# First layer's context attention and feed-forward in a two-layer decoder: another order of a batch's steps

## The chip, the cores and the metric

The kernel runs on one core of a Trainium2 chip, in one launch. The metric is the device time in microseconds (us), from runs of the whole program; lower is better. All arithmetic is in fp32.

Five engines work beside each other, each through its own queue in order: TensorE (PE in the profile; PEld is its weight load), VectorE (DVE), ScalarE (ACT), GpSimd (POOL) and SyncE (SP, which here only issues DMAs). An engine that waits for another holds everything queued behind the waiting instruction. [...]

## The reference

The input is x of 8 batches x 512 tokens x 256, and a context of 8 x 64 x 256 with a mask. Two decoder layers follow, each with self-attention, context attention and a feed-forward part, each part with a residual sum and a layer norm behind it. The change concerns the second and third part of the first layer:

```python
x = _layernorm(x + _L0_xattn_ref(x, ctx_1024, ctx_1024, mask))
#   16 heads of 16; q, k, v are x and the context as they are, no projections:
#   sim = q k^T / sqrt(16) + NEG_BIAS * (1 - mask); out = softmax(sim) v
x = _layernorm(x + _L0_ffn_ref(x, ...))
#   h = gelu(butterfly(x @ W_exp + b_exp) + up_bias)      256 -> 1024
#   y = butterfly(h) @ W_con + b_con + down_bias          1024 -> 256
```

The butterflies are linear; the kernel folds them into the two matrices earlier, so that the feed-forward part is a product with a 256 x 1024 matrix (`wup`), a Gelu, and a product with a 1024 x 256 matrix (`wdn`).

## The kernel before

A batch's 512 tokens are 4 tiles (`NT`) of 128 rows; 256 channels are 2 chunks (`KC`) of 128. The stage `l0_context_ffn` (L1107) works batch after batch in a loop (L1150) with one turn for each (batch, tile). It overlaps two batches: while the context attention of batch b runs, the feed-forward part of batch b-1 or b-2 is taken off a list `pieces`, a few at a time. The order on every engine is that in which the Python code emits the instructions; nothing reorders them.

The steps of the context attention, by their functions:

- `l0x_scores(b, i)` (L700): 8 small products on PE into two PSUM tiles `s_xs` (L708), in an order in which the first two go to the first tile and the next two to the second. Then on DVE two additions of the mask bias, one for each tile (L721), the maximum of each head (L729), and on POOL the subtraction of it (L730). The result is `p`.
- `l0x_exps(b, i)` (L740): one Exp on ACT, in place in `p`. `l0x_sums` (L743): the sums of each head, on DVE (L746).
- `l0x_transposes(b, i)` (L949): 8 transposes of `p` on PE into two PSUM tiles `tP` (L957), each copied by ACT to `pt` (L958).
- `l0x_values(b)` (L960): 8 products on PE for the whole batch into one PSUM tile `s_xpv` (L966), copied by two ACT copies to `oT` (L975); then the context of batch b+2 is fetched by DMA.
- `l0x_back(b)` (L980): 4 reciprocals of the sums on DVE (L985), 8 transposes `tO` on PE (L995), the scaling by the reciprocals on DVE (rx, L997), the residual sum on POOL (rx, L1003), the layer norm's statistics on DVE (L237, L238, then ve at L248) and a power on POOL (L249). The scaling of the layer norm, one short DVE step (ve, L253) and four ACT steps (L257), is put on a list `backs`.
- `l0x_keys(b)` (L692): two POOL operations that spread the context of batch b (bd, L684), a DMA for its mask, and a DVE step for its bias (L154).
- `turned_x(b)` (L672): 8 transposes of x into two PSUM tiles (`tT`, L678), copied by ACT (L679).

The steps of the feed-forward part, from `ffn(b)` (L1008): the transposes of x to `xF`, then 16 pieces. Eight `up` pieces make the first-matrix products, one PSUM tile `s_h` each (4 products of 512 columns, L1015), with a Gelu on ACT behind each (`gate`, L1022). Eight `down` pieces make the second-matrix products into two PSUM tiles `o_out` (L1039); on DVE the residual sum (r, L1049) and the statistics follow; the scaling goes to a list `ends`. `plus` (L1024) is a POOL operation that prepares the residual. `some(n)` takes up to n pieces, `run(queue)` takes the first entry of a list.

PSUM is split (L946) into 2 tiles of two banks (`s`: `s_xs` and `s_xpv`), 3 tiles of one bank (`t`: `tP`, `tO`, `tT`, even `s_h`, first `o_out`) and 1 tile of one bank (`o`: odd `s_h`, second `o_out`). A step that needs a tile waits until its last reader is done:

```python
ctx.enter_context(psum("b", 2, 3, 1))
# in l0x_scores
ss = [s_tile("s_xs") for _ in range(2)]
# in l0x_values
s = s_tile("s_xpv")
```

Exp and Gelu use different tables of ACT, and a table load (`ACT_TABLE_LOAD`) stands in ACT's queue at each change between them; copies and the layer norm's scaling have none. In the loop before, each turn has the scores of one tile, the sums and transposes of the tile before it, two pieces, the Exp, and two more pieces. At tile 0 the turn also has `l0x_values` of the batch before and `l0x_keys` of the next, at tile 1 `l0x_back`, at tile 2 the scaling from `backs`, `turned_x` of the next batch and `ffn`, at tile 3 `plus`.

The stage before this one and the second layer behind it are the same in both kernels. After the loop the rest of `pieces` is run, with the first steps of the second layer among the last twelve.

Of the kernel before, what the change touches and what calls it, by code (L numbers as in the profile page):

```python
# [50 lines left out]
def decoder_kernel(ctx: ExitStack, tc: tile.TileContext, a: dict, out: bass.AP):  # L51
# [640 lines left out]
    def l0x_keys(b):  # L692

        bd = ph.tile([P, KC, 8, S2], F32, tag="bd", name="bd")
        for c in range(KC):
            l0x_spread(b, c, bd[:, c])
        l0x_mask(b)
        l0x_bias(b)

    def l0x_scores(b, i, p=None, by=None):  # L700


        xT, bias = live["xT", b], live["bias", b]
        ss = [s_tile("s_xs") for _ in range(2)]
        for c in range(KC):
            for r in range(4):
                quarter = slice(32 * r, 32 * r + 32)
                pe.matmul(  # L708
                    ss[r // 2][:, r % 2, c * P : (c + 1) * P],
                    lhsT=xT[quarter, c, i * P : (i + 1) * P],  # L710
                    rhs=live["bd", b, c][quarter, 2 * r : 2 * r + 2].rearrange("p h k -> p (h k)"),
                    start=True,
                    stop=True,
                )
        if p is None:
            p = ph.tile([P, 16, S2], F32, tag="p", name="p", bufs=4)
        mx = col("mx16", 16)
        live["p", b, i] = p

        def add(j):  # L720
            dve.tensor_tensor(  # L721
                p[:, 8 * j : 8 * j + 8].rearrange("p (r h) k -> p r h k", r=2),
                ss[j][:, :, 0 : 2 * P].rearrange("p r (h k) -> p r h k", k=S2),
                bias[:, i, :].unsqueeze(1).unsqueeze(1).to_broadcast([P, 2, 4, S2]),
                ALU.add,
            )

        def less():
            dve.tensor_reduce(mx, p, AX.X, ALU.max)  # L729
            (by or pool).tensor_tensor(p, p, mx.unsqueeze(2).to_broadcast([P, 16, S2]), ALU.subtract)  # L730

        if by is None:
            add(0)
            add(1)
            less()
            return None
        add(0)
        return [partial(add, 1), less]
# [4 lines left out]
    def l0x_sums(b, i):  # L743
        if i == 0:
            live["sums", b] = early.tile([P, NT, 16], F32, tag="sums16", name="sums")
        dve.tensor_reduce(live["sums", b][:, i, :], live["p", b, i], AX.X, ALU.add)  # L746
# [202 lines left out]
    def l0x_transposes(b, i):  # L949
        pf = live["p", b, i].rearrange("p h k -> p (h k)")  # L950
        if i == 0:
            live["pt", b] = ph.tile([P, 8, S], F32, tag="pt", name="pt", bufs=1)
        pt = live["pt", b]
        for c in range(2):
            t = t_tile("tP")
            for h in range(4):
                pe.transpose(t[:, h, :], pf[:, (4 * c + h) * P : (4 * c + h + 1) * P], ident)  # L957
            (dve.tensor_copy if b == 0 and c else act.copy)(pt[:, 4 * c : 4 * c + 4, i * P : (i + 1) * P], t)  # L958

    def l0x_values(b):  # L960

        pt = live.pop(("pt", b))
        s = s_tile("s_xpv")
        for c in range(KC):
            for r in range(4):
                pe.matmul(  # L966
                    s[32 * r : 32 * r + 32, c, :],
                    lhsT=live["v2"][:, b % 2, 4 * c + r, :],
                    rhs=pt[:, 2 * r + c, :],
                    start=True,  # L970
                    stop=True,
                )
        oT = ph.tile([P, KC, S], F32, tag="oT", name="oT", bufs=1)
        for c in range(KC):
            act.copy(oT[:, c, :], s[:, c, :])  # L975
        live["oT", b] = oT
        if b + 2 < NB:
            l0x_context(b + 2)
# [128 lines left out]
    with phase("l0_context_ffn") as ph, tc.manual_schedule(engines=ALL):  # L1107
        wdn = ph.tile([P, 8, D], F32, tag="wdn", name="wdn", bufs=1)

        def wdn_piece(f):  # L1110
            t = t_tile("tW")
            for j in range(4):
                pe.transpose(t[:, j, :], wdnT[:, j % 2, (f + j // 2) * P : (f + j // 2 + 1) * P], ident)
            act.copy(wdn[:, f : f + 2, :].rearrange("p f n -> p (f n)"), t.rearrange("p j n -> p (j n)"))

        steps_ = [(b, i) for b in range(NB) for i in range(NT)]
        turn0, turn1, product0, product1, _ = unfinished

        def some(n):
            for _ in range(n):  # L1120
                if pieces:
                    pieces.pop(0)()

        def run(queue):
            if queue:
                queue.pop(0)()

        for n, aside in enumerate((nothing, turn0, turn1, nothing)):
            l0x_transposes(*steps_[n])
            aside()  # L1130
        for _ in parts:
            pass
        product0()
        l0x_values(0)
        product1()
        l0x_back(0)
        l0x_transposes(1, 0)
        for n in range(1, NT - 1):
            for f in range(4 * n - 4, 4 * n, 2):
                wdn_piece(f)  # L1140
            l0x_transposes(1, n)
        l0x_keys(2)
        live["xT", 2] = turned_x(2)
        run(backs)
        dve.tensor_tensor(upb, upb2, upb, ALU.add)
        for n in range(NT - 1):
            l0x_sums(1, n)
        more = [slot(f"gate{n}") for n in range(2)]
        gates = [more[f // 4][:, f % 4 * S : (f % 4 + 1) * S] for f in range(8)]
        for n in range(2 * NT, len(steps_) + 3):  # L1150
            b, i = n // NT, n % NT
            if n == 3 * NT:
                wqT = slot("wqT").rearrange("p (c n) -> p c n", c=KC)
                kd_ku = slot("kd_ku")
                wkdT = kd_ku[:, 0:256].rearrange("p (c n) -> p c n", c=KC)
                wkuT = kd_ku[:, 256:1280]
                wvuT = slot("vu")[:, 0:1024]
                tabs = slot("tabs")
                cs = tabs[:, 0:1024].rearrange("p (t n) -> p t n", t=2)
                causal = tabs[:, 1024:1536]  # L1160
                sp.dma_start(out=wqT, in_=rows(a["at_wqT"]))
                sp.dma_start(out=wkdT, in_=rows(a["at_wkdT"]))
                sp.dma_start(out=wkuT, in_=a["at_wkuT"])
                sp.dma_start(out=wvuT, in_=a["at_wvuT"])

                sp.dma_start(out=cs[:, 0, :], in_=a["rope"][0])
                for h in range(0, P, 32):
                    sp.dma_start(out=cs[h : h + 32, 1, :], in_=a["rope"][1][h ^ 32 : (h ^ 32) + 32, :])
                sp.dma_start(out=causal, in_=a["causal"])
            first = n == 2 * NT  # L1170
            if i == 2:
                run(backs)
            if n < len(steps_):
                l0x_scores(b, i)
            if n <= len(steps_):
                l0x_sums(*steps_[n - 1])
                l0x_transposes(*steps_[n - 1])
            if first:
                ffn(0)
                run(pluses)  # L1180
                run(ends)
            if i == 1:
                run(ends)
            if i == 1 and b > 1:
                l0x_back(b - 1)
            some(2)
            if i == 0:
                l0x_values(b - 1)
            if n < len(steps_):
                l0x_exps(b, i)  # L1190
            if i == 2 and b + 1 < NB:
                live["xT", b + 1] = turned_x(b + 1)
            some(2)
            if i == 0 and b + 1 < NB:
                l0x_keys(b + 1)
            if i == 3:
                run(pluses)
            if i == 2 and b > 1:
                ffn(b - 1)
        since = 0  # L1200
        while len(pieces) > 3 * NT:
            run(pieces)
            since = since + 1 if ends else 0
            if since == 3:
                run(ends)
                run(pluses)
        turned = slot("turned").rearrange("p (two j n) -> p two j n", two=2, j=2)
        sooner = [partial(l1_turn, 0, 0), partial(l1_turn, 0, 1), partial(l1_latent, 0)]
        for c in range(2):
            sooner.extend([partial(l1_query, 0, c), lambda c=c: (l1_key(0, c), l1_rope(0, c))])  # L1210
        run(sooner)
        while pieces:
            run(sooner)
            run(pieces)
# [997 lines left out]
```

## Time and profile before

| | |
|---|---|
| median of 3 runs | 3152.14 us (3150.56 to 3152.29) |
| profiled execution, its own time | 3156.77 us |
| its span, first to last instruction | 3155.1 us |
| granted TensorE clock, mean over the span | 0.990 |
| PE busy | 3063.9 us (97%) |
| DVE / ACT / POOL busy | 1920.7 / 1642.3 / 1101.3 us |
| first and last `s_xs` products of the loop's batches 2 to 7 | about 720.9 to 960.3 us |

Times within the profile are counted from the span's start. A line of the timeline gives the start, the time from there to the end of the merged instructions, the engine, the line of the kernel, the operation, output and inputs, the count, and in brackets the idle time ahead of it and what ended that. [...] An fp32 product of the code appears as two entries in PE's counts. Some matmul records can be missing.

### The profile page before, as it was taken

The page shows a single profiled execution, that of the slowest core. Times are in us where ns is not written, and L with a number is a line of the kernel's source. Part 1 is how long each engine was busy: PE and PEld are TensorE (multiplying, and loading weights), DVE is VectorE, ACT ScalarE, POOL GpSimd, SP SyncE. Part 2 cuts the span into 40 slices and gives each one's busy share as a digit, 9 for nine tenths or more (in the row PEclk, how much of TensorE's full clock was granted, in tenths as well). Part 3 has the DMA queues.
Part 4 walks back from the last instruction along what each step waited for, and adds up shares of the span by engine and source line. Part 5 has one row for each costly group of instructions (what it writes and reads, how often), then busy time and mean ns, then how long its engine had stood idle before and what let it go on. Part 6 is the DMA issues. An engine that isn't in the chain of part 4 may idle for free.

```text
span 3155.1 us, 54217 instructions
## 1 busy us (share of the span) xinstructions
PE 3063.9 (97%) x19598; PEld 2029.3 (64%) x19598; DVE 1920.7 (61%) x6331; ACT 1642.3 (52%) x3507; POOL 1101.3 (35%) x992
## 2 busy tenths in 40 slices
PE   8999999999999999999999999999999999999995
PEld 3444444455666677677767765666666558888885
DVE  6888888876553767767677746766766773110112
ACT  4555555557664666766676656555545543222222
POOL 5988888934432222222222210011111112221222
PEclk8999999999999999999999999999999999999998
DMA  5000111101006963333332310000000016766674
GB/s 165 28 28 28 41 45 44 35 6 43 6 3 170 255 132 48 41 41 41 42 45 38 42 43 1 16 16 25 22 18 21 21 51 210 226 193 180 185 238 148
DMA packets 170975, 235.25 MB, mean 75 GB/s; under 512 B 31915, under 2 KB 134059, under 8 KB 170709
## 3 DMA queue, kind: packets, MB, share of 16 engines
q1 hardware_dynamic: 144692, 179.91, 18.2%
q0 software_dynamic: 25584, 51.57, 11.5%
q8 instruction: 155, 2.54, 0.3%
q14 instruction: 112, 0.91, 0.1%
q10 hardware_dynamic: 432, 0.33, 0.0%
HBM read 136.03 MB, written 61.12 MB: 62 GB/s over the span
## 4 chain that ended last, share of the span: by engine, by line
PE 83%; DVE 6%; ACT 4%; DMA 2%; SPq 2%; issue 1%; POOL 0%; POOLq 0%; DVEq 0%; ACTq 0%
PE o_y L1975 7%; PE s_h L1958 7%; PE s_sc L480 5%; PE s_sc L1560 4%; PE o_pv L1345 4%; PE s_sc L1283 4%; PE tP L1332 4%; PE o_pv L576 4%; PE o_out L1369 4%; PE o_out L1039 3%; PE o_pv L1602 3%; PE s_q L1080 3%; PE o_qkv L1525 3%; PE tP L1592 3%; PE s_h L1015 2%; PE s_st L556 2%
## 5 line engine op out<-in xcount | busy, mean ns | idle before, releaser
L565 ACT ACTIVATE pt<-s_st 128x1024 f32<-128x1024 f32 x256 | 248.3, 1022 | 263.5 <-PE s_st L561 263.5
L1101 POOL DMA_DIRECT2D qk<-turned x256 | 202.8, 1168 | 520.2 <-PE tP L1332 319.4
L489 DVE CUSTOM_DVE_ANT_0 scored<-s_sc,decay 128x512 f32<-128x512 f32 x492 | 314.5, 686 | 54.3 <-PE s_sc L480 52.5
L1310 ACT ACTIVATE p<-p,nm 128x128 f32<-128x128 f32 (+3 forms) x512 | 282.6, 554 | 61.4 <-DVE nm L1296 61.4
L1263 DVE TENSOR_SCALAR p<-p,rsum 128x576 f32<-128x576 f32 (+4 forms) x768 | 297.1, 429 | 13.6
L1296 DVE CUSTOM_DVE_ANT_0 p<-s_sc,tabs 128x128 f32<-128x128 f32 (+3 forms) x512 | 215.6, 487 | 124.9 <-PE s_sc L1283 124.9
L1995 DVE TENSOR_SCALAR y<-o_y,share 128x256 f32<-128x256 f32 x71 | 34.2, 483 | 403.3 <-PE o_y L1975 403.3
L1958 PE MATMUL s_h<-xnT,we 128*128 128x256 f32 (+1 forms) x1248 | 258.8, 361 | 0.0
L1975 PE MATMUL o_y<-we,h 128*128 128x256 f32 x1136 | 251.4, 379 | 0.0
L1996 POOL DMA_INDIRECT total<-y,to x71 | 109.8, 1546 | 386.2 <-DVE y L1995 193.4
L1570 ACT ACTIVATE p<-s_sc,nm 128x576 f32<-128x576 f32 x256 | 187.4, 737 | 101.8 <-DVE nm L1564 101.1
L1975 PEld LDWEIGHTS o_y<-we,h 128*128 128x128 f32 x1136 | 215.3, 190 | 29.0
L1958 PEld LDWEIGHTS s_h<-xnT,we 128*128 128x128 f32 x1248 | 215.4, 190 | 23.9 <-ACT xnT L1937 0.2
L1564 DVE TENSOR_REDUCE nm<-s_sc 128x1 f32<-128x576 f32 x256 | 181.4, 750 | 73.2 <-PE s_sc L1560 73.2
L1332 PEld LDWEIGHTS tP<-ident,p 128*128 128x128 f32 x1280 | 144.8, 141 | 82.6 <-PE s_sc L1283 41.7
L480 PE MATMUL s_sc<-k,q 32*128 32x512 f32 x1024 | 188.9, 648 | 6.0 <-DVE mx L489 4.9
L1794 POOL DMA_INDIRECT rows_in<-z,irow x64 | 63.2, 988 | 374.2 <-DVE hit L1789 267.1
L1560 PE MATMUL s_sc<-k,q 64*128 64x288 f32 x1024 | 174.2, 433 | 9.7 <-ACT p L1570 9.7
L1332 PE MATMUL tP<-ident,p 128*128 128x128 f32 x1280 | 175.2, 276 | 0.1
L1937 ACT ACTIVATE xnT<-tZ,gb 128x256 f32<-128x256 f32 (+1 forms) x78 | 42.6, 546 | 237.5 <-PE tZ L1936 237.5
L1283 PE MATMUL s_sc<-qk 64*128 64x128 f32 (+3 forms) x1024 | 157.5, 443 | 3.8 <-DMA qk<-turned 3.3
L1965 ACT ACTIVATE h<-s_h 128x1024 f32<-128x1024 f32 x71 | 72.7, 1024 | 155.7 <-PE s_h L1958 155.7
(341 smaller groups left out, 6456.0 us busy)
## 6 DMA issues: line engine op xcount, KB each, us to landing
we<-in_mo_w SPq DMA_DIRECT2D x78, 1024.0 KB
rows_in<-zero SPq DMA_DIRECT2D x64, 530.0 KB
qk<-turned POOLq DMA_DIRECT2D x256, 128.0 KB, 4.3
coef<-in_ff_upw SPq DMA_DIRECT2D x40, 256.0 KB
coef<-in_ff_dnw SPq DMA_DIRECT2D x40, 256.0 KB
xr<-rows_in SPq DMA_DIRECT2D x32, 265.0 KB
x<-in_x SPq DMA_DIRECT2D x8, 512.0 KB
total<-x SPq DMA_DIRECT2D x8, 512.0 KB
```

The costliest lines, as they stand in the source:

```text
L480: pe.matmul(pairs[h // 2][:, h % 2, :], lhsT=q[r, i * P : (i + 1) * P], rhs=k[r, :], start=True, stop=True)
L489: dve.tensor_tensor_reduce(out=rows_[h], in0=pairs[h // 2][:, h % 2, :], in1=decay[:, i, :], scale=1.0, scalar=-3.0e38, op0=ALU.mult, op1= ...
L565: act.activation(pt, s, AF.Exp, scale=1.0 / 16.0)
L1101: pool.dma_start(out=qk[h : h + 32], in_=other[g : g + 32], accum_op=ALU.add)
L1263: dve.tensor_scalar(p[:, j, 0:n], p[:, j, 0:n], rsum[:, j : j + 1], None, ALU.mult)
L1283: pe.matmul(ss[j][:, at : at + n], lhsT=qk[h : h + 64, 0, i * P : (i + 1) * P], rhs=qk[h : h + 64, 1, 0:n], start=True, stop=True,)
L1296: dve.tensor_tensor_reduce(out=p[:, j, :], in0=ss[j], in1=causal[:, S - (i + 1) * P : S], scale=-1.0 / 8.0, scalar=3.0e38, op0=ALU.add, op ...
L1310: act.activation(p[:, j, :], p[:, j, :], AF.Exp, bias=nm[:, j : j + 1], scale=-1.0, accum_out=sums[:, j : j + 1])
L1332: pe.transpose(t[:, n, :], p[:, j, at * P : (at + 1) * P], ident)
L1560: pe.matmul(s[:, t, :], lhsT=q[h : h + 64, i * P : (i + 1) * P], rhs=k[h : h + 64, at : at + HALF], start=True, stop=True)
L1958: pe.matmul(s[:, j, :], lhsT=w1[:, c, f * P : (f + 1) * P], rhs=xnT[:, c, :], start=(c == 0), stop=(c == KC - 1),)
L1975: pe.matmul(o, lhsT=h[:, f, i * P : (i + 1) * P], rhs=w2[:, f, :], start=(f == 0), stop=(f == 7),)
```

## The change

The loop over (batch, tile) becomes a loop over batches with the order of a batch written out. In the first half of a batch the last two transposes of the batch before, then the four score steps of this batch, with the eight `up` pieces, `l0x_values`, `l0x_keys` and `l0x_back` among them; then `turned_x` and the four exponentials, one behind the other. In the second half four `down` pieces, the transposes of tiles 0 and 1 with the other four `down` pieces around them, `ffn` and `plus`, and the sums of tiles 2 and 3. The products, tiles and buffers are the same.

```diff
         gates = [more[f // 4][:, f % 4 * S : (f % 4 + 1) * S] for f in range(8)]
-        for n in range(2 * NT, len(steps_) + 3):
-            b, i = n // NT, n % NT
-            if n == 3 * NT:
+        for b in range(2, NB + 1):
+            if b == 3:
                 wqT = slot("wqT").rearrange("p (c n) -> p c n", c=KC)
...
                 sp.dma_start(out=causal, in_=a["causal"])
-            first = n == 2 * NT
-            if i == 2:
-                run(backs)
-            if n < len(steps_):
-                l0x_scores(b, i)
-            if n <= len(steps_):
-                l0x_sums(*steps_[n - 1])
-                l0x_transposes(*steps_[n - 1])
-            if first:
+            own = [partial(l0x_scores, b, i) for i in range(NT)] if b < NB else [nothing] * NT
+            if b == 2:
+                own[0]()
+                l0x_sums(1, NT - 1)
+                l0x_transposes(1, NT - 1)
                 ffn(0)
                 run(pluses)
                 run(ends)
-            if i == 1:
-                run(ends)
-            if i == 1 and b > 1:
-                l0x_back(b - 1)
+            else:
+                for i in range(2, NT):
+                    l0x_transposes(b - 1, i)
+                own[0]()
             some(2)
-            if i == 0:
-                l0x_values(b - 1)
-            if n < len(steps_):
+            l0x_values(b - 1)
+            own[1]()
+            some(2)
+            if b + 1 < NB:
+                l0x_keys(b + 1)
+            run(ends)
+            l0x_back(b - 1)
+            own[2]()
+            some(2)
+            own[3]()
+            some(2)
+            if b + 1 < NB:
+                live["xT", b + 1] = turned_x(b + 1)
+            if b == NB:
+                run(backs)
+                some(4)
+                ffn(b - 1)
+                break
+            for i in range(NT):
                 l0x_exps(b, i)
-            if i == 2 and b + 1 < NB:
-                live["xT", b + 1] = turned_x(b + 1)
+            some(4)
+            l0x_sums(b, 0)
+            l0x_transposes(b, 0)
+            run(backs)
             some(2)
-            if i == 0 and b + 1 < NB:
-                l0x_keys(b + 1)
-            if i == 3:
-                run(pluses)
-            if i == 2 and b > 1:
-                ffn(b - 1)
+            l0x_sums(b, 1)
+            l0x_transposes(b, 1)
+            some(2)
+            ffn(b - 1)
+            run(pluses)
+            for i in range(2, NT):
+                l0x_sums(b, i)
         since = 0
```

## The prediction

> **What bounds the kernel now.** First the page: which engine is full, and what the chain of waits that ended last consists of.
>
> ```profile
> PE 3063.9 (97%) x19598; PEld 2029.3 (64%) x19598; DVE 1920.7 (61%) x6331; ACT 1642.3 (52%) x3507; POOL 1101.3 (35%) x992
> PE 83%; DVE 6%; ACT 4%; DMA 2%; SPq 2%; issue 1%; POOL 0%; POOLq 0%; DVEq 0%; ACTq 0%
> ```
>
> TensorE (PE) is full and carries 83% of the chain. An edit that only reorders can gain no more than PE's idle time in the stretch that it reorders. That stretch runs from about 724 to 985 us. Next the busy time by windows, one window of 43 us in it (columns: window, length, then busy us of PE, PEld, DVE, ACT, POOL, then the granted clock, DMA share, GB/s), and the groups of ScalarE's table loads over 724 to 985:
>
> ```profile
> 767.00:810.00 43.00, 41.73 (x238) 27.12 (x236) 25.08 (x50) 29.36 (x41) 18.12 (x13) 1.00 0.03 5
> L1022 ACT ACT_TABLE_LOAD x19 | 24.4, 1283 | 7.0 <-PE s_h L1015 6.7
> L741 ACT ACT_TABLE_LOAD x18 | 23.1, 1283 | 0.3
> ```
>
> PE lacks 1.27 us in 43, ACT 13.64. ACT's 37 table loads (six a batch) are mostly off the path. Where PE waits is seen in PE's timeline of one batch:
>
> ```profile
> 769.25 1.92 PE L966 MATMUL s_xpv<-pt,v 128*32 128x512 f32 x16
> 771.10 3.70 PE L1015 MATMUL s_h<-xF,wup 128*128 128x512 f32 x8
> 774.73 0.73 PE L708 MATMUL s_xs<-bd,xT 32*128 32x128 f32 x16
> 775.39 1.09 PE L957 MATMUL tP<-ident,p 128*128 128x128 f32 x8
> 776.79 0.65 PE L995 MATMUL tO<-ident,oT 128*128 128x128 f32 x4 [0.31 <-ACT gate L1022]
> 777.84 0.66 PE L995 MATMUL tO<-ident,oT 128*128 128x128 f32 x4 [0.40 <-ACT pt L958]
> 778.33 7.13 PE L1015 MATMUL s_h<-xF,wup 128*128 128x512 f32 x16
> 786.05 1.09 PE L957 MATMUL tP<-ident,p 128*128 128x128 f32 x8
> 787.71 3.72 PE L1039 MATMUL o_out<-wdn,gate 128*128 128x256 f32 x16 [0.57 <-ACT gate L1022]
> 810.27 1.92 PE L966 MATMUL s_xpv<-pt,v 128*32 128x512 f32 x16
> ```
>
> A batch is 810.27 - 769.25 = 41.02 us. I read an operation's price as the distance to the next start. Eight tP cost 0.93 us where nothing is waited for (797.22 to 798.15), but 1.40 at 775.39 and 1.66 at 786.05; the first four tO cost 1.05, the second four 0.49. Waits of a batch: 0.47 + 0.56 + 0.73 = 1.76 us. All three are ACT being late with a PSUM tile, behind an exponential between two table loads. PE's own work is 41.02 - 1.76 = 39.26 us.
>
> **The change, part by part.** No instruction of PE, DVE or POOL is added or removed; ACT loses four of its six table loads a batch, 4 x 1.283 = 5.1 us.
>
> *Gain.* The exponentials no longer stand among the first-matrix products, so the three old waits can go: 1.76 us a batch, at most. What is late next is the pair of `s` tiles that a score step fills: there are only two such tiles, a step takes both, and s_xpv takes one. In the new order these steps stand closer together.
>
> *First new wait.* Score step 1 now follows s_xpv directly; before, two first-matrix pieces (3.6 us) lay between. Its second tile is the one that s_xpv filled and that ACT's two copies must empty:
>
> ```profile
> 771.29 1.07 ACT L975 COPY oT<-s_xpv 128x512 f32<-128x512 f32 x2 [1.05 <-PE s_xpv L966]
> ```
>
> The copies end at 772.36, 3.11 us after s_xpv's start, and PE follows 0.05 later (as after the gates above). PE would be there after 1.85 + 0.16 (the four of sixteen products that go to the free tile) = 2.01. Wait: 3.16 - 2.01 = 1.15 us. No row shows this pair of steps back to back. Bounds: 0.6, if one copy were enough; 1.7, if ACT came one gate (0.6) later.
>
> *Second new wait.* Step 3 needs step 2's additions, and on DVE these stand behind the whole of `l0x_back`: bias, ve, reciprocals, rx and statistics. The statistics wait for POOL's two sums rx, which stand behind step 1's subtraction and the two bd of `l0x_keys`. The rows:
>
> ```profile
> 775.49 1.29 DVE L721 TENSOR_TENSOR p<-s_xs,bias 128x512 f32<-128x512 f32 x2 [4.46 <-PE s_xs L708]
> 776.81 1.22 DVE L729 TENSOR_REDUCE mx<-p 128x16 f32<-128x1024 f32 x1
> 783.77 0.43 DVE L237 BATCH_NORM_STATS2 st<-rx 128x6 f32<-128x256 f32 x1
> 784.98 0.17 DVE L248 TENSOR_SCALAR ve<-mv 128x4 f32<-128x4 f32 x1
> ```
>
> ```profile
> 772.75 2.04 POOL L684 TENSOR_TENSOR bd<-ctxT,small 128x512 f32<-128x512 f32 x2
> 778.11 1.90 POOL L730 TENSOR_TENSOR p<-p,mx 128x1024 f32<-128x1024 f32 x1 [3.32 <-DVE mx L729]
> 781.25 2.50 POOL L1003 TENSOR_TENSOR rx<-rx,x 128x512 f32<-128x512 f32 x2 [1.23 <-DVE rx L997]
> ```
>
> Count from the end of step 1 on PE (775.39 in the old order). Maximum out: 778.03 - 775.39 = 2.64. Subtraction out: 780.01, so 4.62. Two bd: 6.66. Two sums rx: 9.16. The last two statistics and ve take 784.98 - 783.77 = 1.21 after the second sum, plus 0.05 and 0.08 between the steps: step 2's additions start at 10.50. The first is out after 0.68, the second 0.64 later; with 0.05 each, the tiles are free at 11.23 and 11.87. PE's way: two pieces 3.53, tO 0.95, step 2 0.66, two pieces 3.53, so 8.67 for the first tile and 8.83 for the second. Wait: 11.87 - 8.83 = 3.04 us. DVE's other work in this time is covered by POOL: a ve step held up by POOL's subtraction (0.96 us at 779.08 against 0.17 at 786.35, both ending with POOL's operation) ends at 4.65, reciprocals 0.5 and the first rx 0.68 make 5.8, before bd ends at 6.66. Bounds: 2.0 if one bd (1.02) were out of the way, 4.1 if one more stood in it.
>
> *Costed at nothing.* s_xpv needs the first tile of step 0. From the last second-matrix product, DVE takes 5.9 (r, statistics, then two sums of 1.13 that are now ahead, then an addition), plus 0.2 to start; PE takes xF 0.93, sixteen tP 1.86, step 0 0.66, two pieces 3.53 = 6.98. Slack 0.85; if gone, the excess is paid. The four exponentials: step 3's subtraction ends 5.1 after step 3 on PE, ACT's copies of xT at 5.6, one load and four exponentials to 11.1; PE comes to the first tP at 11.5, and needs only the first exponential (7.9). The scaling from `backs` (2.07) has 7.9 us of products before xF. Six PSUM tiles in a row at the batch's start go out at ACT's 0.535 against PE's 0.46: 0.1. The mask and context DMAs on SP keep their order and become due later than the tile they reuse; the layer-1 loads stay at the head of the fourth batch. After the loop the same 12 pieces are left.
>
> *Sum.* New waits 1.15 + 3.04 + 0.10 = 4.29, less 1.76: +2.5 us a batch. From s_xpv at 728.23 to that at 972.75 there are six batches. The last has no bd and no bias: POOL's sums start when tO and rx are out (about 5.0 after step 1, against 6.66), so some 1.7 less, +0.8. Five times 2.5 and 0.8: +13.3 us. The profiled execution took 3156.77 us (span 3155.1 plus 1.7 around it), and would take 3170.1; it lies 4.6 above the median of the runs, 3152.14, to which I add the same: 3165.4.
>
> [...]
>
> The granted clock is 1.00 in all rows of this stretch, with no PE wait over 0.6 us in the batch shown; 2.5 us in one piece is new here. [...]
>
> **The rivals.** (1) Faster: the two `s` tiles are emptied in time, so the old waits go and no new one comes. Both new waits are for these tiles; it decides when the copies oT end 1.15 us and step 2's additions 3.04 us sooner than counted. Gain 1.66 x 6 = 10, so 3142. For it: ACT is the releaser of all three old waits. Against: DVE's and POOL's order is written out, and no row in the sum is faster elsewhere. (2) No difference: only the first wait comes, because POOL's rx sums are ahead of what I count: 1.15 + 0.10 - 1.76 = -0.5, six times -3, so 3149. (3) Worse: the 2.5 us gap lowers the clock, or a ve step held by POOL runs behind both bd. The second holds rx until 6.66 + 0.5 + 0.7 = 7.9 and moves the sums by 1.2; the clock was granted at 0.90 from 40 to 80 us, where PE idled 1.7 us in 40, and 4% less for a batch would be 1.7. Together 1 to 3 more a batch: 3171 to 3183.
>
> **How the numbers follow.** Forecast 0.80, rival 1 0.04, rival 2 0.07, rival 3 0.09. The bounds of the waits (2.6 to 5.8 a batch, less 1.76, six times) reach from +5 to +24; both at an end together is unlikely. Range 3158 to 3172: +1.0 to +3.3 a batch, which leaves rivals 1 and 2, and most of 3. About 0.2% (6.3 us) is what a measurement of this kernel can tell from no change: faster 0.04, same 0.08, slower 0.88.
>
> **What would show it.** Right: the s_xpv starts of the changed kernel lie 43.5 us apart; the second half of a score step after s_xpv waits 1.1 us for ACT oT; the fourth step of a batch waits about 2.5 and then 0.5 us for DVE's additions; tO and the first o_out wait for nothing; ACT has 12 or 13 table loads in the stretch where there were 37. Wrong: starts of s_xpv under 41 us apart, a granted clock under 1.00 there, or a difference that lies behind 985 us.

## The result, and the profile after

The changed kernel takes 3168.57 us (median of 6 runs, 3166.9 to 3173.9) against 3152.22 of the kernel before in the same comparison (6 runs, 3150.07 to 3155.93): 16.4 us more, a ratio of 1.0056, 95% interval 1.0046 to 1.0066. In the experiments below the same kernel, run once more, gave 1.0072 (1.0058 to 1.0085).

The totals of the profile say nothing of the cause: PE is as full as it was, and ACT has lost 29.5 us of work.

```profile
PE 3066.8 (97%) x19598; PEld 2032.5 (64%) x19598; DVE 1915.1 (61%) x6331; ACT 1612.8 (51%) x3483; POOL 1099.8 (35%) x992
```

The groups of table loads from 724 to 1000 us show the intended part done, 12 loads where there were 37:

```profile
L741 ACT ACT_TABLE_LOAD x6 | 7.7, 1283 | 0.1
L1022 ACT ACT_TABLE_LOAD x6 | 7.7, 1283 | 10.6 <-PE s_h L1015 10.6
```

The waits of PE over the same stretch. The old releasers (gate, pt) are gone, and only readers of the two `s` tiles are left:

```profile
PE s_xs L708 <- DVE p L721: 11.5, 6, 2.2
PE s_xs L708 <- ACT oT L975: 5.0, 6, 0.8
```

The windows from one s_xpv to the next (columns as before the change). A batch was 41.02 us; the granted clock is the third column from the end:

```profile
721.01:764.13 43.12, 40.09 (x234) 27.09 (x233) 25.92 (x53) 22.92 (x36) 18.43 (x13) 1.00 0.24 75
764.13:808.93 44.80, 41.70 (x234) 28.00 (x233) 22.29 (x46) 23.11 (x37) 16.40 (x11) 0.96 0.03 5
808.93:855.21 46.28, 43.29 (x233) 28.52 (x233) 22.29 (x46) 23.11 (x37) 16.40 (x11) 0.93 0.03 5
...
944.92:985.07 40.15, 38.46 (x209) 25.73 (x209) 21.37 (x43) 22.15 (x35) 14.10 (x9) 1.00 0.00 1
```

The first of these batches is slower by 2.10 us at full clock, the next four by 3.8 to 5.3 at a lowered one. The six windows sum to 264.06 us, 19.5 more than the 244.52 before. At 43.12 for each of the first five it would be +11.2, so the clock has 8.3 us of it. The two profiled executions differ by less, 10.1 us of span, because the one of before was granted a clock of only 0.90 in its first 100 us, where the one of after had 1.00, in code that is the same in both: its first s_xpv came at 708.59 us, this one's at 701.38. The other 2.2 us lie behind the last s_xpv, in a stretch that took between 2178.9 and 2187.8 us in the profiles of this case.

One batch on PE, the one with the lowest clock:

```profile
808.93 1.92 PE L966 MATMUL s_xpv<-pt,v 128*32 128x512 f32 x16
810.78 0.49 PE L708 MATMUL s_xs<-bd,xT 32*128 32x128 f32 x4
812.10 0.71 PE L708 MATMUL s_xs<-bd,xT 32*128 32x128 f32 x12 [0.83 <-ACT oT L975]
...
817.90 3.70 PE L1015 MATMUL s_h<-xF,wup 128*128 128x512 f32 x8
823.76 1.82 PE L708 MATMUL s_xs<-bd,xT 32*128 32x128 f32 x16 [2.16 <-DVE p L721]
825.51 6.29 PE L1015 MATMUL s_h<-xF,wup 128*128 128x512 f32 x8
```

The four score products that go to the free tile run at once, the twelve others 3.17 us after s_xpv's start. Step 3 could start at 817.90 + 3.53 (two pieces, from start to next start) = 821.43 and starts at 823.76. The two pieces behind it, which take 3.53 us elsewhere, take 6.13: the clock is at 0.50 from 824 until about 830.8 us. Two of the rows that show it (the clock again third from the end):

```profile
824.00:825.00 1.00, 1.00 (x14) 0.79 (x14) 0.97 (x2) 0.00 (x0) 0.28 (x1) 0.50 0.00 0
830.00:831.00 1.00, 1.00 (x3) 0.47 (x2) 0.00 (x0) 0.08 (x1) 0.05 (x1) 0.62 0.00 0
```

The chain that holds step 3, on POOL and then on DVE:

```profile
815.36 1.90 POOL L730 TENSOR_TENSOR p<-p,mx 128x1024 f32<-128x1024 f32 x1 [3.59 <-DVE mx L729]
817.22 2.05 POOL L684 TENSOR_TENSOR bd<-ctxT,small 128x512 f32<-128x512 f32 x2
819.22 2.49 POOL L1003 TENSOR_TENSOR rx<-rx,x 128x512 f32<-128x512 f32 x2
```

```profile
820.52 0.43 DVE L237 BATCH_NORM_STATS2 st<-rx 128x6 f32<-128x256 f32 x1 [2.26 <-POOL rx L1003]
...
823.03 1.28 DVE L721 TENSOR_TENSOR p<-s_xs,bias 128x512 f32<-128x512 f32 x2
```

POOL works from 815.36 to 821.71 without a pause; DVE stands 2.26 us for it, and step 2's additions come after that.

### The profile page after: what moved, and what is told of

Same layout as the page of the kernel before. It is cut to its first block, busy times and chain, and to the rows that moved or that the text cites. A ratio compares the mean times of both kernels' runs of the same rounds, so it can differ in the third digit from the quotient of the medians.

```text
span 3165.2 us, 54242 instructions
## 1 busy us (share of the span) xinstructions
PE 3066.8 (97%) x19598; PEld 2032.5 (64%) x19598; DVE 1915.1 (61%) x6331; ACT 1612.8 (51%) x3483; POOL 1099.8 (35%) x992
## 4 chain that ended last, share of the span: by engine, by line
PE 85%; DVE 6%; ACT 3%; issue 1%; DMA 1%; POOL 1%; POOLq 0%; ACTq 0%; DVEq 0%; SPq 0%
PE s_h L1972 7%; PE o_y L1989 7%; PE s_sc L480 5%; PE o_pv L1359 5%; PE s_sc L1297 5%; PE tP L1346 4%; PE s_sc L1574 4%; PE o_pv L576 4%; PE o_out L1383 4%; PE o_pv L1616 4%; PE o_out L1039 3%; PE s_q L1080 3%; PE o_qkv L1539 3%; PE tP L1606 3%; PE s_h L1015 3%; PE s_st L556 2%
## 5 line engine op out<-in xcount | busy, mean ns | idle before, releaser
L1359 PE MATMUL o_pv<-pt,vc 128*64 128x128 f32 (+1 forms) x2304 | 153.5, 287 | 0.0
```

The lines of the kernel that those rows point to most:

```text
L1359: pe.matmul(o[64 * j : 64 * (j + 1), cols], lhsT=v[:, k, 64 * j : 64 * (j + 1)], rhs=pt[:, j, n : n + len(block), :].rearrange("p k n -> p ...
```

## The experiments

Theory A: the two waits for the `s` tiles, and a clock that falls because of the longer of them. Theory B: the order by halves is slow in itself, or ACT's table loads still matter. Theory C: the clock falls for another reason than that wait. The kernel before had a median of 3150.75 us beside the first four kernels, 3149.5 beside the second four, 3149.38 beside the last three.

**1. The bd operations behind step 3.**

```diff
-            if b + 1 < NB:
-                l0x_keys(b + 1)
             run(ends)
             l0x_back(b - 1)
             own[2]()
             some(2)
             own[3]()
+            if b + 1 < NB:
+                l0x_keys(b + 1)
```

> The two bd operations and the bias of the next batch are emitted behind score step 3 instead of ahead of the back step. Theory A (the second new wait is the chain subtraction, two bd, two sums rx, statistics, additions of step 2; the lowered clock follows from the length of that gap): the chain is 1.8 us shorter (2.04 of bd, of which 0.2 comes back because rx is out only then), the wait in front of step 3 falls from about 2.9 to about 1.1 us, the clock stays at 1.00 in every batch; s_xpv starts 41.3 us apart; 3151 to 3154 us, about the kernel before. Theory B (the order of the halves itself is slow: exponentials, transposes and pieces come late, and DVE stands still for other reasons): the wait moves elsewhere, the time stays near 3168. Theory C (the lowered clock has nothing to do with the gap): 9 us less from the wait, clock still 0.96 in four batches, about 3160.

Measured: 3154.04 us, ratio 1.0015 (1.0005 to 1.0025); s_xpv 41.72 to 41.78 us apart, clock 1.00 in every batch. Step 3's wait on PE:

```profile
818.37 1.31 PE L708 MATMUL s_xs<-bd,xT 32*128 32x128 f32 x16 [0.75 <-DVE p L721]
```

A holds: taking 2.04 us of POOL out of the chain takes 1.4 us out of the batch against 43.12, and the clock's loss with it. PE is there at 817.45 and starts at 818.37, and another 0.6 goes between the two tiles: 1.5 us, 0.4 more than I had worked out.

**2. Step 2 ahead of the back step.**

```diff
             run(ends)
-            l0x_back(b - 1)
             own[2]()
+            l0x_back(b - 1)
             some(2)
```

> Score step 2 is emitted ahead of the back step, so that its additions stand ahead of the statistics on DVE. Theory A: the second wait goes whole (about 2.9 us a batch), with it the lowered clock; only the wait of step 1 behind s_xpv (1.15) stays; s_xpv 40.2 us apart against 41.0 in the kernel before; 3146 to 3149 us, a little under the kernel before. Theory B: still well over 3152. Theory C: clock 0.96 in four of the batches, about 3155.

Measured: 3147.16 us, ratio 0.9983 (0.9974 to 0.9993); s_xpv 40.32 us apart, clock 1.00. The waits for DVE are gone from PE's list, those for oT stand as they were (5.0 us in 6). One step moved ahead of another (on PE, DVE and POOL alike) turns a loss of 0.6% into a gain of 0.2%: B falls.

**3. Unread products in the gap, and 9 to 11: the same again beside the changed kernel.**

```diff
             own[2]()
             some(2)
+            if b < NB:
+                filler = t_tile("filler").rearrange("p i n -> p (i n)")
+                for c in range(KC):
+                    pe.matmul(filler, lhsT=wup[:, c, 0:P], rhs=live["xT", b][:, c, :], start=(c == 0), stop=(c == KC - 1))
             own[3]()
```

> Everything as in the changed kernel, with one extra group of first-matrix products (about 1.8 us of PE work, result not read) in front of score step 3, in the gap in which PE waits for DVE's additions. Theory A: step 3 starts when it did, the idle part of the gap falls from 2.3 to about 0.6 us, the clock stays 1.00; s_xpv 43.1 us apart in all batches; 3161 to 3165 us, some 5 to 8 us less than the changed kernel although PE does more. Theory C (the clock falls for another reason, such as the small score products or heat): clock 0.93 to 0.96 as before, 3168 or more.

Measured: 3165.84 us, ratio 1.0051 (1.0039 to 1.0064); s_xpv 43.12 to 43.19 apart, clock 1.00 in all batches:

```profile
821.96 1.88 PE L1194 MATMUL filler<-xT,wup 128*128 128x512 f32 x4
824.28 1.31 PE L708 MATMUL s_xs<-bd,xT 32*128 32x128 f32 x16 [0.45 <-DVE p L721]
825.52 3.70 PE L1015 MATMUL s_h<-xF,wup 128*128 128x512 f32 x8
```

Step 3 starts as late as in the changed kernel, and the pieces behind it are fast again. By the trace C falls. The time, a little above the expected 3161 to 3165 us, does not show it against the changed kernel, whose interval (1.0046 to 1.0066) overlaps; so three kernels were run side by side: the changed kernel unaltered,

> The changed kernel once more, beside the kernels with a filled gap on the same chip, to see how much of its time is the lowered clock. In its profile the waits cost 11.2 us and the clock 8.3. If both stand in every run: 18 to 20 us over the kernel before (1.0058 to 1.0064); if the clock falls less often in other runs: 12 to 17 us.

the filled gap,

> The kernel with about 1.8 us of unread products in the gap once more, on the same chip. Clock theory: clock 1.00, 11 to 12 us over the kernel before (1.0036), 3 to 8 us under the changed kernel of this call. Rival: the same time as the changed kernel, since its waits are the same.

and half of the filler (only c = 0).

> Half the filler: one product of 512 columns, about 0.9 us, in front of score step 3; the gap's idle part falls from 2.3 to about 1.4 us. If the clock follows from an idle stretch of over 2 us: clock 1.00 in all batches, the same time as with the whole filler. If a stretch of about 3.4 us with little work in it suffices: the clock still falls in some batches, between the two others.

Measured: 3172.16 us, ratio 1.0072 (1.0058 to 1.0085), for the changed kernel, with a lowered clock in each of its first five batches; 3164.81 us, 1.0052 (1.0038 to 1.0066), for the filled gap, 1.00 everywhere; 3163.44 us, 1.0045 (1.0031 to 1.0059), for half the filler. The changed kernel is 22.8 us over the kernel before, more than either expectation had, and the filled gap 15.4, where 11 to 12 was expected. The filled gap is 7.4 us under the changed kernel beside it, which does less work; the intervals overlap by a little, so the size of the clock's part in the time is known only to some microseconds (8.3 and 10.0 us in the two profiles).

Half the filler gave no clean answer. The clock still fell in three of five batches (44.82, 44.88 and 44.89 us against 43.17 and 43.18), although PE's idle stretch was only 1.23 to 1.30 us:

```profile
821.86 1.02 PE L1193 MATMUL filler<-xT,wup 128*128 128x512 f32 x2
824.18 1.31 PE L708 MATMUL s_xs<-bd,xT 32*128 32x128 f32 x16 [1.30 <-DVE p L721]
825.41 5.40 PE L1015 MATMUL s_h<-xF,wup 128*128 128x512 f32 x8
```

"Over 2 us" is wrong. The other expectation, that the clock still falls in some batches, came true, but the time did not lie between the two others: it is slightly under both, so the times do not show what the three falls cost. With 0.45 (filled gap), 0.75 (experiment 1) or 0.83 us of idle time (the wait for oT in each batch) it never fell.

The length of the gap does not decide alone. Here PE is idle from 822.88 to 824.18 and the clock falls at 826.28, 2.1 us later. Read in slices of 0.1 us from 720 to 1000 us, the first profile of the changed kernel has four falls, at 779.56, 823.93, 871.72 and 916.09, which end at 782.97, 830.76, 875.13 and 919.50. The seven later times all lie whole multiples of 3.413 us behind the first, to 0.03 us (1, 13, 15, 27, 28, 40 and 41 steps). So in this profile the changes stand on a grid. Steps of it, two neighbours and one more, then two stretches of half the filler that are as long, 13 steps apart (length, then PE's busy time):

```profile
731.77:735.19 3.42, 1.92 (x5) 0.57 (x3) 2.43 (x10) 1.37 (x2) 1.95 (x2) 1.00 0.83 235
735.19:738.60 3.41, 2.71 (x20) 1.69 (x21) 3.38 (x5) 0.00 (x0) 1.90 (x2) 1.00 0.00 0
776.15:779.56 3.41, 1.14 (x6) 0.30 (x5) 3.15 (x11) 0.69 (x1) 1.78 (x2) 1.00 0.00 0
778.50:781.91 3.41, 2.00 (x15) 0.81 (x15) 3.18 (x10) 0.69 (x1) 1.46 (x2) 1.00 0.00 0
822.87:826.28 3.41, 2.01 (x19) 1.31 (x19) 3.31 (x7) 0.00 (x0) 1.18 (x2) 1.00 0.00 0
```

The third and the fifth end in a fall. In the batch of the changed kernel that was spared, the end of a step lies within the gap (the first two rows, 1.50 and 0.70 us idle). Of the steps of this profile from 721 to 988 us, the four at whose end the clock fell had 1.85 to 2.27 us of idle time, and no other more than 1.50. The last two rows, equal in idle time (1.41 and 1.40), end differently. They differ in what PE was busy with: 0.81 us of it is score products in the first, 1.20 in the second. In the profile of the changed kernel PE was busy with other things than score products for 0.09 to 1.08 us in the four steps ahead of a fall and for 1.34 or more in all others; no run tested whether that decides.

**4. Three moves: step 2 ahead of the back step, bd behind step 3, one piece between s_xpv and step 1.**

```diff
             l0x_values(b - 1)
+            some(1)
             own[1]()
-            some(2)
-            if b + 1 < NB:
-                l0x_keys(b + 1)
+            some(1)
             run(ends)
-            l0x_back(b - 1)
             own[2]()
+            l0x_back(b - 1)
             some(2)
             own[3]()
+            if b + 1 < NB:
+                l0x_keys(b + 1)
```

> Three moves together: one first-matrix piece between s_xpv and score step 1 (the other behind it), score step 2 ahead of the back step, bd and bias behind step 3. Theory A: both new waits go and the old ones stay away; s_xpv 39.3 us apart; 3140 to 3143 us, about 10 us (0.3%) under the kernel before. Theory B: the order of the halves has a cost of its own, not under 3152.

Measured: 3139.34 us, ratio 0.9968 (0.9957 to 0.9979): faster than both kernels. A batch takes 39.22 us, all of it PE's work; no step waits:

```profile
802.64 1.92 PE L966 MATMUL s_xpv<-pt,v 128*32 128x512 f32 x16
804.49 1.98 PE L1015 MATMUL s_h<-xF,wup 128*128 128x512 f32 x4
806.41 0.73 PE L708 MATMUL s_xs<-bd,xT 32*128 32x128 f32 x16
...
841.86 0.64 PE L966 MATMUL s_xpv<-pt,v 128*32 128x512 f32 x4
```

**5 and 6. No table load, in the order of before and in that of after.** Tanh stands for Gelu in the feed-forward part of the first layer, so this function is another one.

```diff
-            act.activation(gates[f], s, AF.Gelu, bias=upb[:, f : f + 1])
+            act.activation(gates[f], s, AF.Tanh, bias=upb[:, f : f + 1])
```

> The kernel before with Tanh in the place of Gelu in the first layer's feed-forward part: the build then has no table load in the loop, the order is that of before. It sizes the gain that the change was credited with. If the three old waits (1.76 us a batch) come from the table loads around the exponentials: s_xpv 39.3 to 39.6 us apart, 3141 to 3144 us. Rival: they come from the order of the copies and transposes, and 41.0 stays: 3152.

Measured: 3145.11 us, ratio 0.9983 (0.9974 to 0.9993); s_xpv 40.05 us apart. The loads are worth 0.97 us of the 1.76 a batch, about half of what I had credited them with. The old waits go, but two smaller ones come in their place, 0.19 us for rx and 0.20 for a gate; the other 0.4 us stands in no listed wait.

> The changed kernel with Tanh in the place of Gelu: no table load in the loop. The two loads left in a batch are off the path if the waits of the changed kernel are DVE's and POOL's: 3166 to 3170 us, both waits as they were. Rival (ACT still sets the pace): 1.3 to 2.6 us a batch less, 3153 to 3161.

Measured: 3170.36 us, ratio 1.0069 (1.0056 to 1.0081), both waits as they were (2.2 and 0.8 us at the longest). In the order of after the last twelve loads cost nothing that the profile or the time shows. The clock fell in all of the first five batches.

**7. The bd operations twice.**

```diff
-    def l0x_keys(b):
+    def l0x_keys(b, times=1):
...
-        for c in range(KC):
+        for c in [*range(KC)] * times:
             l0x_spread(b, c, bd[:, c])
...
             if b + 1 < NB:
-                l0x_keys(b + 1)
+                l0x_keys(b + 1, 2)
```

> The changed kernel with the two bd operations made twice (2.04 us more on POOL, a batch), at their place. Theory A: the wait in front of step 3 grows by 2.0 us a batch in five batches (10 us), and the longer gap lowers the clock in all of them, by as much as in the worst batch so far (3.2 us): 3180 to 3188 us. Rival (POOL's chain is not the one that ends last): 3168 to 3171.

Measured: 3185.15 us, ratio 1.0110 (1.0096 to 1.0124), clock 0.93 in five batches of 47.59 to 47.78 us:

```profile
791.99 1.82 PE L708 MATMUL s_xs<-bd,xT 32*128 32x128 f32 x16 [4.15 <-DVE p L721]
793.74 5.74 PE L1015 MATMUL s_h<-xF,wup 128*128 128x512 f32 x8
```

Two more bd on POOL are 2.0 us more in front of step 3: POOL's chain is the one that ends last.

**8. One piece between s_xpv and step 1, alone.**

```diff
             l0x_values(b - 1)
+            some(1)
             own[1]()
-            some(2)
+            some(1)
```

> The changed kernel with one of the two first-matrix pieces moved from behind score step 1 to ahead of it. The first new wait (1.15 us) goes, but step 1's chain starts one piece (1.77) later while PE comes to step 3 at the same distance less one piece: the second wait grows from 2.9 to about 4.7 us. Theory A: +0.6 us a batch in waits, and the longer gap lowers the clock in each batch: 3172 to 3179 us. Rival (the two waits are independent): 7 us less than the changed kernel, 3162.

Measured: 3177.95 us, ratio 1.0092 (1.0079 to 1.0105). The wait for oT is gone from the list, step 3's has grown to 4.1 us, clock 0.93 to 0.96 in all six batches. Curing the first wait alone makes the kernel slower, by 9.4 us against the changed kernel's first median and 5.8 against its second (its interval overlaps the second one's a little): the piece that covers s_xpv is taken away from the cover of step 3.

## Why the prediction was right, and where it was not

The sign, the range (3158 to 3172 against 3168.57) and the two waits held; the forecast was +13.3 us, the measurement +16.4. One of the prediction's own signs of being wrong came, a granted clock under 1.00 in the loop. That the sum still came close is partly luck: it had 2 us too much in the waits (13.3 against 11.2) and none of the clock's 8.3, and the same kernel run once more, 3172.16 us, lies just outside the range. Step by step:

- **Gain.** The three old waits went whole: tO and the first o_out wait for nothing. Experiment 5 shows that they were only in part the table loads': without the loads, but in the old order, half of them stays.
- **First new wait.** Worked out 1.15 us, measured 3.17 - 2.01 = 1.16.
- **Second new wait.** From the end of step 1 (812.74) the chain was worked out as 4.62, 6.66, 9.16 and 10.50 us for subtraction, bd, rx and step 2's additions; it was 4.52, 6.53, 8.97 and 10.29. PE was there after 8.69 (8.67). Wait for the first tile 2.33 us against 2.56 worked out. I had let POOL hold up the ve step; it did not (0.15 us at 815.33, ahead of the subtraction). As written, POOL covered that place either way. With the second tile, in the first batch at full clock, the wait cost 2.84 us against 3.04 worked out.
- **Sum of a batch.** +2.5 worked out, +2.1 to 2.2 at full clock (43.12 to 43.19, where the clock stays up). The last batch: +0.8 worked out, 0.74 measured (40.15 against 39.41).
- **The term that was mis-sized: the clock.** I put it at nothing and left it to rival 3. No run shows that a gap of 2.5 us costs nothing. The clock fell in four batches of one profile of the changed kernel and in five of the other, after 2.1 or 2.2 us of idle time, and a fall cost 1.7 us, or 3.2 in the worst batch. Rival 3 also had 1.7 a batch, but from a clock 4% lower, which no row gave: that the two agree is luck. The step that failed is costing at nothing a gap that was, in the prediction's words, "new here". With waits of +11.2 and a clock of +8.3 the profile has 19.5 us; the measured 16.4 lies between the waits alone and that.
- **Costed at nothing and so found:** the exponentials (834.87 to 838.76, the first tP at 839.42), the scaling, the additions ahead of s_xpv, and the tail behind the loop, where PE runs the same products at the same distances in both kernels over its first 50 us.
- **Rivals.** Rival 1 needed both tiles free in time. Experiment 4 makes that true by order alone and gains 11.4 us where 10 were named. Rival 2 (3149) needed POOL's sums earlier; with the bd out of their way, experiment 1 gave 3154. Of rival 3 the lowered clock came, and the ve step held by POOL did not.

The table loads were gathered as intended, and ACT lost 29.5 us. In the order of before, doing without any load was worth 1.0 us a batch to the path (experiment 5), and the new order took back more than that: from 41.02 to 43.12 us a batch at full clock.

## What to carry to other kernels

Before steps are gathered to save switches on an engine that has time to spare, list the PSUM tiles that the gathered steps share, and follow in every queue what stands ahead of each tile's last reader. Here step 2's additions stood behind a layer norm that waits for POOL, and moving one call cured it (43.12 to 40.32 us a batch, experiment 2). A wait of 2.2 us on the full TensorE cost 1.7 or 3.2 us beyond its length, because the clock fell behind it: so look at the granted clock of each batch, not of the whole run. And where two waits depend on one pair of tiles, look at both after each cure: experiment 8 filled the first and took the cover from the second, while experiment 2 cured the second alone and gained.

## What the runs showed of the hardware

- In the first profile of the changed kernel the granted clock fell to 0.50 in four of the five batches with an idle stretch of 2.1 to 2.2 us on PE and stayed there for 3.4 us (779.56 to 782.97, and twice more) or twice that (823.93 to 830.76), so a fall cost 1.7 or 3.2 us. The falls and their ends stood on a grid of 3.413 us, and in the spared batch the end of a step lay within the gap. In the second profile it fell in five of five.
- With an idle stretch of 1.23 to 1.30 us (half the filler) it fell in 3 of 5 batches; in the batches whose idle stretches were at most 0.83 and 0.45 us (the filled gap) or 0.83 and 0.75 us (experiment 1) it never fell. What the grid starts from is not known: the fall at 826.28 with half the filler lies 13.7 steps behind 779.56.
- The first 100 us, the same code, were granted 0.90, 0.97 or 1.00 in different profiled executions. The two with 0.90 came to the first s_xpv at 707.9 and 708.6 us, the others between 697.7 and 704.6. A comparison of two single profiles is off by some microseconds for that; a batch against a batch is not.
